# Two graph layers with routed experts on one core: bf16 one-hot rows added before counting, the input normalized on ScalarE, and the first pass reordered

## The chip, the cores and the metric

The kernel runs on one core of a Trainium2 chip. The metric is the device time of one execution in microseconds (us); lower is better. The engines of a core are TensorE (PE; its weight loads are listed as PEld), VectorE (DVE), ScalarE (ACT), GpSimd (POOL) and SyncE (SP). Each works through its own queue in order and waits on semaphores for the others.

## The reference

The input `x` is (128, 64, 256), that is 8192 tokens of 256 numbers in 128 graphs of 64 nodes, with one adjacency matrix a graph. Two layers follow; each normalizes first and adds a residual.

```python
x = x + gnn0(layernorm(x), adj)     # (eps*x + adj@x) @ W1 + b1, rms norm, silu, @ W2 + b2  (256 -> 1024 -> 256)
x = x + ffn0(layernorm(x))          # top 6 of 64 experts, each a 256x256 matrix, softmax weights,
                                    # then a projection, a residual and a layernorm
x = x + gnn1(layernorm(x), adj)     # layernorm, adj@h, two products, relu, residual
x = x + ffn1(layernorm(x))          # top 2 of 8 experts, each 256 -> 512 -> 256 with relu
```

## The kernel before

The kernel makes four passes. The first does `gnn0`, chooses the experts of `ffn0` and writes each token, with its weight and its destination, into rows of a table in DRAM that belong to the chosen expert (until about 700 us). The second fetches pages of 128 rows of one expert each, multiplies them and sends the products back. The third does the rest of `ffn0`, `gnn1` and the routing of `ffn1`; the fourth does the experts of `ffn1`.

The first pass works on 32 blocks of 256 tokens (`T = 2` tiles of 128). `staggered` takes a list of (lag, stage) pairs and in step `s` calls each stage, in the order of the list, for block `s - lag`. So one step holds parts of five blocks: norm and aggregation of block `s+1`, the hidden layer of block `s`, the second product (`project`) of block `s-1`, the residual, second norm, transposes (`turn`) and expert logits (`gate`) of block `s-2`, and the choice and the sending of block `s-3`. PE, DVE and ACT execute in exactly the order in which the stages are written. The framework orders the queues of POOL and SP itself.

The stages that matter here, with the lines of the profile:

- `norm_a`, `norm_s`, `norm_b`: statistics of the input on DVE (L45, L46), reciprocal deviation on ACT (`rstd`, L58, L59), normalized input on DVE (L573). `norm_e` adds the scaled identity to the adjacency tile (L563).
- `hidden(b, j)`, four times: products into one of four PSUM buffers `ph` (L591), then the square of each into `sq` on ACT (L594). `square_sum` adds the eight squares up as a tree on DVE (L601). `rms` sums over partitions on PE (L605), takes the reciprocal root on ACT and loads the table for silu. `scale` multiplies on DVE (L613) and applies silu on ACT (L615).
- `residual_a`, `residual_s`, `residual_b`: residual and statistics on DVE (L630), then six normalized copies of the block, one for each chosen expert, into `xs` (three buffers) on ACT (L643), and two stores.
- `choose`: the eight largest logits and their positions on DVE (L178, L179), then one-hot rows for the six choices (`hot`, 2 x 6 x 64 a partition, L183) by comparing float positions with a table of expert numbers. `weigh` prepares the softmax (L242 on DVE, L243 on ACT) and lets POOL write the destinations (L240).
- `count`: for each of the six choices a product with a strictly upper triangular matrix and one with ones (L191), which count the earlier tokens of each expert.
- `place`: softmax division (`normalize`), bookkeeping, row numbers, 12 sends. The bookkeeping gives experts new chunks of rows once every four blocks: `move_on`, `grow` and `note` run with the blocks whose number is 0, 1 and 2 modulo 4, from block 4 on. Then the counts become places (L267 to L275), the one-hot rows pick each token's row (L277 product, L279 sum, L281 cast) and POOL issues 12 indirect sends (L287).

Three bias rows are split into three bf16 parts each by `row_parts` before the first block (L469 to L476), so that a product with ones can add them. `load_lattice` loads a part of the expert matrices in each of 16 steps.

```python
        staggered(NB, (
            (3, choose), (2, residual_a), ..., (0, lambda b: hidden(b, 0)), (0, lambda b: hidden(b, 1)),
            (2, residual_s), (-1, norm_s), (-1, norm_e), (3, weigh),
            (0, lambda b: hidden(b, 2)), (0, lambda b: hidden(b, 3)), (3, count), (2, residual_b), (-1, norm_b), ...
```

Of the kernel before, what the change touches and what calls it, by code (L numbers as in the profile page):

```python
# [78 lines left out]
class Router:  # L79
# [15 lines left out]
    def __init__(self, tc, pool, small, dram, n, D, E, K, T, pg, S, epoch, name, total=None):  # L95
# [3 lines left out]
        self.epoch, self.EP, self.pitch = epoch, epoch * T * P, S + pg  # L99
# [8 lines left out]
        assert T == 2 and epoch == 4 and n % self.EP == 0 and S % pg == 0 and (5 * T * P <= S or S >= n)  # L108
# [5 lines left out]
        self.expert = self.iota([P, 2 * E], [[1, 2 * E]], 0, "expert")  # L114
        self.page = self.iota([P, 4], [[1, 4]], 4, "page")
# [56 lines left out]
    def choose(self, logits):  # L172

        nc, T, E, K, n = self.nc, self.T, self.E, self.K, self.name
        top = self.small.tile([P, T, 8], F32, name=n + "top")
        idx = self.small.tile([P, T, 8], U32, name=n + "idx")
        for t in range(T):
            nc.vector.max(top[:, t, :], logits[:, t, :])  # L178
            nc.vector.max_index(idx[:, t, :], top[:, t, :], logits[:, t, :])  # L179
        which = self.small.tile([P, T, K], F32, name=n + "which")  # L180
        nc.vector.tensor_copy(which, idx[:, :, :K])
        hot = self.work.tile([P, T, K, E], BF16, name=n + "hot")
        nc.vector.tensor_tensor(hot, self.expert[:, :E].unsqueeze(1).unsqueeze(1).to_broadcast([P, T, K, E]),  # L183
                                which.unsqueeze(3).to_broadcast([P, T, K, E]), op=ALU.is_equal)
        return top, hot

    def count(self, hot):

        for m, lhsT in enumerate((self.tri, self.ones)):
            for k in range(self.K):  # L190
                self.nc.tensor.matmul(self.psum[:, m], lhsT=lhsT, rhs=hot[:, :, k, :],  # L191
                                      start=(k == 0), stop=(k == self.K - 1))
# [15 lines left out]
    def grow(self):  # L208

        v, E = self.nc.vector, self.E  # L210
        t, new, cum = self.t, self.new, self.cum
        v.tensor_sub(t, self.end, self.run[:, 0, :])
        v.scalar_tensor_tensor(new, t, float(self.EP), self.none, op0=ALU.is_lt, op1=ALU.mult)
        v.tensor_tensor_scan(cum, new, self.zero[:, :E], self.used, op0=ALU.add, op1=ALU.add)
        v.tensor_copy(self.used, cum[:, E - 1:E])
        v.tensor_scalar(cum, cum, -1.0, float(self.pitch), op0=ALU.add, op1=ALU.mult)
        v.tensor_sub(t, cum, self.end)
        v.tensor_sub(t, t, self.delta)
        v.tensor_mul(t, t, new)
        v.tensor_add(self.delta, self.delta, t)  # L220
        v.tensor_sub(self.none, self.none, new)
# [37 lines left out]
    def places(self, b, hot):  # L259

        nc, T, E, K, n = self.nc, self.T, self.E, self.K, self.name
        if self.J > 1 and b >= self.epoch and b % self.epoch < 3:
            (self.move_on, self.grow, self.note)[b % self.epoch]()
        pos, cnt = self.psum[:, 0], self.psum[:, 1]
        run = self.run
        self.run = self.counts.tile([P, T, E], F32, name=n + "run")
        nc.vector.tensor_add(run[:, 1, :], run[:, 0, :], cnt[:, 0, :])  # L267
        nc.vector.tensor_add(self.run[:, 0, :], run[:, 1, :], cnt[:, 1, :])
        place = self.work.tile([P, T, E], F32, name=n + "place", bufs=1)
        nc.vector.tensor_add(place, pos, run)  # L270
        if self.J > 1:
            over = self.work.tile([P, T, E], F32, name=n + "over", bufs=1)
            nc.vector.tensor_tensor(over, place, self.end.unsqueeze(1).to_broadcast([P, T, E]), op=ALU.is_ge)
            nc.vector.tensor_mul(over, over, self.delta.unsqueeze(1).to_broadcast([P, T, E]))
            nc.vector.tensor_add(place, place, over)  # L275
        prod = self.work.tile([P, T, K, E], F32, name=n + "prod", bufs=1)
        nc.vector.tensor_mul(prod, hot, place.unsqueeze(2).to_broadcast([P, T, K, E]))  # L277
        row = self.small.tile([P, T, K], F32, name=n + "rowf")
        nc.vector.tensor_reduce(row, prod, op=ALU.add, axis=AX.X)  # L279
        out = self.small.tile([P, T, K], I32, name=n + "row")  # L280
        nc.vector.tensor_copy(out, row)  # L281
        return out
# [129 lines left out]
def two_layer_gnn_moe_kernel(ctx: ExitStack, tc: tile.TileContext, a: dict, out: bass.AP):  # L412
# [49 lines left out]
    def row_parts(pool, name):  # L462

        rest = pool.tile([P, D], F32, name="rest_" + name, bufs=1)
        nc.scalar.dma_start(out=rest, in_=rows_of(a[name]))
        part = small.tile([P, D], BF16, name="part", bufs=1)
        out = const.tile([P, 2, D], BF16, name="p_" + name)
        for i in range(3):
            nc.vector.tensor_copy(part, rest)  # L469
            nc.vector.tensor_sub(rest, rest, part)  # L470
            if i == 0:
                nc.vector.tensor_scalar(out[:, 0, :], part, ident[:, 0:1], None, op0=ALU.mult)
            else:
                nc.vector.scalar_tensor_tensor(out[:, 0, :], part, ident[:, i:i + 1], out[:, 0, :],
                                               op0=ALU.mult, op1=ALU.add)
        nc.vector.tensor_copy(out[:, 1, :], out[:, 0, :])  # L476
        return out
# [20 lines left out]
    r0 = Router(tc, const, small, dram, N, D, E0, K0, T, P, 14 * P, 4, "r0")  # L498
# [22 lines left out]
    with tc.tile_pool(name="c0", bufs=1) as c0, \  # L521
# [27 lines left out]
        rms_w = load_columns(c0, "L0_gnn_rms_weight")  # L549
        w2 = w2_view  # L550
        nc.scalar.dma_start(out=w2, in_=a["L0_gnn_W2"].rearrange("(k p) f -> p k f", p=P))
        gate_wT = load_matrix(c0, "L0_ffn_gate_wT")
        b2 = row_parts(c0, "L0_gnn_b2")
        out_b = row_parts(c0, "L0_ffn_out_b")
        b_rel = row_parts(c0, "L1_gnn_b_rel")

# [10 lines left out]

        def norm_b(b):
            B = blocks[b]
            x, mv, rs = B["x"], B["mv"], B["rs"]  # L570
            B["xn"] = xn = pair[:, b % 2 * T:(b % 2 + 1) * T, :]
            for t in range(T):
                nc.vector.tensor_scalar(xn[:, t, :], x[:, t, :], mv[:, t, 0:1], rs[:, t:t + 1],  # L573
                                        op0=ALU.subtract, op1=ALU.mult)
# [34 lines left out]
        def scale(b):  # L609
            B = blocks[b]  # L610
            B["hT"] = hT = hTs[b % 2]
            for c in range(KH):
                nc.vector.scalar_tensor_tensor(hT[:, c, :], B["ph", c // 2][:, c % 2, :], b1[:, c:c + 1], B["rms"],  # L613
                                               op0=ALU.add, op1=ALU.mult)
                nc.scalar.activation(hT[:, c, :], hT[:, c, :], AF.Silu, scale=rms_w[:, c:c + 1])  # L615
            nc.scalar.preload_act_table_set("natural_log_exp_and_others")

        def project(b, t, lo, hi):
            B = blocks[b]
            if t == 0 and lo == 0:  # L620
                B["po"] = psum.tile([P, T, D], F32, name="ps")
                nc.tensor.matmul(B["po"], lhsT=r0.ones, rhs=b2, start=True, stop=False)
# [12 lines left out]

        def residual_b(b):
            B = blocks[b]
            x1, mv, rs = B["x1"], B["mv1"], B["rs1"]
            nm = small.tile([P, T], F32, name="bn_nm")
            nc.vector.scalar_tensor_tensor(nm, mv[:, :, 0], -1.0, rs, op0=ALU.mult, op1=ALU.mult)  # L640
            B["xs"] = xs = work.tile([P, T, K0, W], F32, name="xs", bufs=3)
            for t in range(T):
                nc.scalar.activation(xs[:, t, :, :D], x1[:, t, :].unsqueeze(1).to_broadcast([P, K0, D]),  # L643
                                     AF.Identity, bias=nm[:, t:t + 1], scale=rs[:, t:t + 1])
            nc.sync.dma_start(out=by_tile(x1_dram[b]), in_=x1)
# [9 lines left out]
        def gate(b):  # L655
            B = blocks[b]
            for t in range(T):
                for k in range(KD):
                    nc.tensor.matmul(pg[:, t, :], lhsT=B["xn1T"][:, k, ts(t, P)], rhs=gate_wT[:, k, :],
                                     start=(k == 0), stop=(k == KD - 1))  # L660

        def choose(b):
            B = blocks[b]
            B["top"], B["hot"] = r0.choose(pg)
# [5 lines left out]
        def count(b):  # L670
            r0.count(blocks[b]["hot"])

        def place(b):
            B = blocks[b]
            r0.normalize(*B["w"], B["xs"])
            r0.send(r0.places(b, B["hot"]), B["xs"])

        def load_lattice(b):
            n = free[0] // 16
            if b < 16:  # L680
                nc.sync.dma_start(out=lat[:, b * n:(b + 1) * n], in_=lat_w[:, b * n:(b + 1) * n])
# [11 lines left out]
            (-1, norm_e),  # L693
            (3, weigh),
            (0, lambda b: hidden(b, 2)),
            (0, lambda b: hidden(b, 3)),
            (3, count),
            (2, residual_b),
            (-1, norm_b),
            (1, lambda b: project(b, 0, 0, 4)),  # L700
            (0, square_sum),
            (-1, aggregate),
            (1, lambda b: project(b, 0, 4, KH)),
            (2, turn),
            (0, rms),
            (3, place),
            (1, lambda b: project(b, 1, 0, KH)),
            (2, gate),
            (0, scale),
            (1, load_lattice),  # L710
# [68 lines left out]
    with tc.tile_pool(name="c3", bufs=1) as c3, \  # L779
# [43 lines left out]
        def out_proj(b):  # L823
            B = blocks[b]
            B["pp"] = pp = po_pool.tile([P, T, D], F32, name="po")
            nc.tensor.matmul(pp, lhsT=r1.ones, rhs=out_b, start=True, stop=False)  # L826
# [68 lines left out]
        def convolve_a(b):  # L895
            B = blocks[b]
            B["pc"] = pc = po_pool.tile([P, T, D], F32, name="pc")
            nc.tensor.matmul(pc, lhsT=r1.ones, rhs=b_rel, start=True, stop=False)  # L898
# [40 lines left out]
        def choose1(b):  # L939
# [3 lines left out]
            top, B["hot"] = r1.choose(logits)  # L943
            r1.compare(b, top, B["xs"])

        def count1(b):
            r1.count(blocks[b]["hot"])
# [5 lines left out]
        def place1(b):  # L953
            B = blocks[b]
            r1.send(r1.places(b, B["hot"]), B["xs"])
# [122 lines left out]
```

## Time and profile before

| | |
|---|---|
| median of 3 runs | 2195.01 us (2194.39 to 2196.17) |
| profiled execution | 2200.25 us, its span 2198.1 us |
| mean granted TensorE clock | 0.962 |
| busy PE / PEld | 88% / 77% of the span |
| busy DVE / ACT / POOL | 54% / 46% / 54% |
| DMA | 398.93 MB, 181 GB/s on average |

The rows of the profile's views give, for a group of instructions, the start, the duration, the engine, the line, the operation and `output<-input` by the tiles' names, with shapes as partitions x elements, and in brackets the idle time before it with what ended that. An `x8` behind a row says that eight like it are merged; the duration is then that of all eight. The view by groups gives a mean in ns. Idle time of an engine that nothing waits for costs nothing. `lat` is a large SBUF tile in which several arrays of the first pass live (`x`, `sq`, `hT`, W1, W2), so many rows name it.

### The profile page before, as it was taken

To read this page: it belongs to the slowest core of one execution; us is meant where nothing else is said; L and a number is where in the kernel's file an instruction comes from. 1 tells how busy PE (TensorE), PEld (TensorE's weight loads), DVE (VectorE), ACT (ScalarE), POOL (GpSimd) and SP (SyncE) were. 2 spreads that over 40 slices of the span, in tenths; PEclk is the share of its full clock that TensorE was granted. 3 is DMA by queue.
4 is the path that set the end of the run, shared out by engine and by line. 5 is a ranking of instruction groups with operands and counts; after the bars stand their busy time and mean duration, and the time that the engine had idled before them with its cause. 6 is when DMAs were issued, how large, how long until landed. Compare 5 with 4: busy or idle time off the path is not lost. (4 is left out here: it accounts for less than half of the span.)

```text
span 2198.1 us, 37431 instructions
## 1 busy us (share of the span) xinstructions
PE 1945.1 (88%) x10563; PEld 1684.8 (77%) x10564; DVE 1186.6 (54%) x3904; ACT 1015.9 (46%) x2037; POOL 1182.8 (54%) x1178
## 2 busy tenths in 40 slices
PE   3999999999961988998898479999996999999997
PEld 2888888888851877887777368888875888888886
DVE  4688888888873333333333248888882222222221
ACT  2887887777750222222222036666662333333332
POOL 1166676666655777777777703333343444434444
PEclk9999999999985999999999789999997999999999
DMA  8143334443364988767675379888835776666665
GB/s 247 56 133 123 129 131 134 133 133 134 127 214 136 282 254 256 210 202 206 206 206 170 92 277 316 265 265 267 262 124 142 179 170 158 162 157 161 162 160 117
DMA packets 283580, 398.93 MB, mean 181 GB/s; under 512 B 56024, under 2 KB 237416, under 8 KB 283376
## 3 DMA queue, kind: packets, MB, share of 16 engines
q1 hardware_dynamic: 200736, 246.15, 38.3%
q0 software_dynamic: 64800, 136.14, 20.8%
q10 hardware_dynamic: 17840, 14.21, 2.0%
q8 instruction: 93, 1.52, 0.3%
q14 instruction: 111, 0.91, 0.2%
HBM read 223.89 MB, written 177.69 MB: 183 GB/s over the span
## 5 line engine op out<-in xcount | busy, mean ns | idle before, releaser
L287 POOL DMA_INDIRECT r0x<-xs,r0row x384 | 397.7, 1036 | 222.2 <-DVE lat L613 100.7
L294 POOL DMA_INDIRECT r0y<-py_s,px x424 | 417.6, 985 | 143.7 <-DMA r0y<-py_s,px 58.2
L758 PE MATMUL py<-lat,pxT 128*128 x1696 | 411.0, 385 | 40.0 <-DVE py_s L763 22.5
L763 DVE TENSOR_SCALAR py_s<-py,px 128x256 f32<-128x256 f32 x424 | 185.6, 479 | 377.4 <-DMA r0y<-py_s,px 158.5
L302 POOL DMA_INDIRECT out_x<-py_s,px x138 | 214.4, 1554 | 312.1 <-DMA out_x<-py_s,px 184.2
L758 PEld LDWEIGHTS py<-lat,pxT 128*128 128x128 f32 x1696 | 307.2, 191 | 91.0 <-issue 31.2
L745 ACT COPY pxT<-pt 128x512 f32<-128x512 f32 x212 | 124.0, 586 | 440.8 <-PE pt L743 309.5
L1017 ACT ACTIVATE phid<-ph,pw 128x256 f32<-128x256 f32 x276 | 131.0, 475 | 325.3 <-issue 178.4
L1015 PE MATMUL ph<-pxT,pw 128*128 128x256 f32 x1104 | 251.4, 381 | 2.1 <-DMA pw<-in_L_ffn_W1b 2.1
L1034 PE MATMUL py<-fw,phid 128*128 x1104 | 249.9, 379 | 0.6 <-ACT phid L1017 0.6
L591 PE MATMUL ph<-lat 128*128 128x256 f32 x1024 | 233.2, 387 | 17.8 <-DVE lat L613 17.1
L624 PE MATMUL ps<-lat 128*128 128x256 f32 x1024 | 237.1, 380 | 0.0
L1015 PEld LDWEIGHTS ph<-pxT,pw 128*128 128x128 f32 x1104 | 211.0, 191 | 31.4 <-issue 2.5
L591 PEld LDWEIGHTS ph<-lat 128*128 128x128 f32 x1024 | 195.2, 193 | 46.9 <-DVE lat L613 17.4
L1034 PEld LDWEIGHTS py<-fw,phid 128*128 128x128 f32 x1104 | 204.4, 190 | 26.0 <-ACT phid L1017 1.0
L624 PEld LDWEIGHTS ps<-lat 128*128 128x128 f32 x1024 | 192.8, 191 | 24.5
L287 POOL DMA_INDIRECT r1x<-xs,r1row x128 | 129.8, 1014 | 115.7 <-ACT xn3T L930 61.9
L743 PE MATMUL pt<-ident,px 128*128 128x128 f32 x848 | 131.8, 277 | 45.0 <-DMA px<-r0x 44.7
L743 PEld LDWEIGHTS pt<-ident,px 128*128 128x128 f32 x848 | 106.8, 143 | 70.9 <-issue 42.9
L1028 DVE TENSOR_SCALAR p<-p 128x2 f32<-128x2 f32 x69 | 12.0, 174 | 240.1 <-ACT p L1027 240.1
L1037 DVE TENSOR_TENSOR py_s<-py,pb 128x512 f32<-128x512 f32 x69 | 47.7, 692 | 157.0 <-PE py L1034 152.0
L615 ACT ACTIVATE lat<-lat,c_L_gnn_rms_weight 128x256 f32<-128x256 f32 x256 | 105.6, 495 | 47.8 <-DVE lat L613 47.7
(264 smaller groups left out, 2866.7 us busy)
## 6 DMA issues: line engine op xcount, KB each, us to landing
px<-r0x SPq DMA_DIRECT2D x424, 129.0 KB
y<-r0y SPq DMA_DIRECT2D x32, 1536.0 KB
pw<-in_L_ffn_W1b SPq DMA_DIRECT2D x69, 514.0 KB
px<-r1x SPq DMA_DIRECT2D x69, 258.0 KB
x<-x SPq DMA_DIRECT2D x64, 256.0 KB
pb<-in_L_ffn_b SPq DMA_DIRECT2D x69, 128.0 KB
r0x<-r0filler ACTq DMA_DIRECT2D x64, 129.0 KB
lat<-in_x SPq DMA_DIRECT2D x32, 256.0 KB
```

The costliest lines, as they stand in the source:

```text
L287: i = self.nc.gpsimd.indirect_dma_start(out=self.table[:, :], out_offset=bass.IndirectOffsetOnAxis(ap=row[:, t, k:k + 1], axis=0), in_=xs[ ...
L294: i = self.nc.gpsimd.indirect_dma_start(out=self.answer[:, :], out_offset=bass.IndirectOffsetOnAxis(ap=x[:, self.D:self.D + 1].bitcast(I32 ...
L302: i, d = f"{self.name}add{i}", self.nc.gpsimd.indirect_dma_start(out=self.total[:, :], out_offset=bass.IndirectOffsetOnAxis(ap=x[:, self.D ...
L591: nc.tensor.matmul(ph[:, c, :], lhsT=w1[:, k, ts(2 * j + c, P)], rhs=B["aggT"][:, k, :], start=(k == 0), stop=(k == KD - 1))
L624: nc.tensor.matmul(B["po"][:, t, :], lhsT=B["hT"][:, c, ts(t, P)], rhs=w2[:, c, :], start=False, stop=(t == T - 1 and c == KH - 1))
L743: nc.tensor.transpose(pt[:, k, ts(q, P)], Q["px", q][:, 0, ts(k, P)], ident)
L745: nc.scalar.copy(xT[:, :, :n * P], pt[:, :, :n * P])
L758: nc.tensor.matmul(py[:, q, :], lhsT=Q["xT"][:, k, ts(q, P)], rhs=lat[:, ds(regs["e"][(2 * j + q) % 4], 1), k, :].rearrange("p o d -> p (o ...
L763: nc.vector.tensor_scalar(y[:, q, :], py[:, q, :], px[:, 0, D + 1:D + 2], None, op0=ALU.mult)
L1015: nc.tensor.matmul(ph, lhsT=w[:, k * F1 + c * P:k * F1 + (c + 1) * P], rhs=Q["xT"][:, k, :], start=(k == 0), stop=(k == KD - 1))
L1017: nc.scalar.activation(hid[:, c, :], ph, AF.Relu, bias=w[:, KD * F1 + c:KD * F1 + c + 1], scale=1.0)
L1034: nc.tensor.matmul(py[:, t, :], lhsT=Q["hid"][:, c, ts(t, P)], rhs=fw2[:, ds(regs["e"][i % 4], 1), c, :].rearrange("p o d -> p (o d)"), st ...
```

## The change

The diff does the following to the shared router and to the first pass.

1. `choose` compares in bf16 with a table `experts` whose last dimension repeats each number three times (`half = K // 2`); the one-hot rows are laid out as 2 x 64 x 3. It then adds the six rows up (`some`, `its`), and `count` makes one product with each matrix instead of six (one instead of two for the second router).
2. The bookkeeping is spread over four blocks: `grow` is cut in two, its second half being `link`, and `note` moves to the blocks that are 3 modulo 4. The room that is kept for an expert grows from four to five blocks, and the chunk of the first router falls from 14 to 13 pages.
3. `place` is cut in two: `spots` (softmax division, bookkeeping, places) stays ahead of the scaling, and `place` (row numbers and sends) goes behind it.
4. The input's normalization moves to ACT, with a small DVE operation for its shift (`norm_n`). The shift of the second norm gets a stage of its own as well (`residual_n`).
5. Of the six copies of a block the first is made in `residual_b`, which now stands between `hidden(b, 2)` and `hidden(b, 3)`; the other five are made by `normalized` behind `norm_b` and behind `aggregate`.
6. `rms` is called ahead of `turn`.
7. The bias rows, W2, the rms weights and the gate weights are loaded after the first `aggregate` (`load_late`), and one row is split in each of the first three steps (`split_late`). `load_lattice` runs eight steps later.

```diff
-        self.epoch, self.EP, self.pitch = epoch, epoch * T * P, S + pg
+        self.epoch, self.EP, self.pitch = epoch, (epoch + 1) * T * P, S + pg
...
+        self.experts = pool.tile([P, E, self.half], BF16, name=name + "experts")
+        nc.vector.tensor_copy(self.experts, self.expert[:, :E].unsqueeze(2).to_broadcast([P, E, self.half]))
...
-        which = self.small.tile([P, T, K], F32, name=n + "which")
-        nc.vector.tensor_copy(which, idx[:, :, :K])
-        hot = self.work.tile([P, T, K, E], BF16, name=n + "hot")
-        nc.vector.tensor_tensor(hot, self.expert[:, :E].unsqueeze(1).unsqueeze(1).to_broadcast([P, T, K, E]),
-                                which.unsqueeze(3).to_broadcast([P, T, K, E]), op=ALU.is_equal)
+        which = self.small.tile([P, T * 2, h], BF16, name=n + "which")
+        nc.vector.tensor_copy(which.rearrange("p (t a) c -> p t (a c)", t=T), idx[:, :, :K])
+        hot = self.work.tile([P, T, 2, E, h], BF16, name=n + "hot")
+        nc.vector.tensor_tensor(hot.rearrange("p t a e c -> p (t a) e c"),
+                                self.experts.unsqueeze(1).to_broadcast([P, T * 2, E, h]),
+                                which.unsqueeze(2).to_broadcast([P, T * 2, E, h]), op=ALU.is_equal)
+        some = self.work.tile([P, T, E, h], BF16, name=n + "some", bufs=1)
+        nc.vector.tensor_add(some..., hot[:, :, 0]..., hot[:, :, 1]...)
+        its = self.work.tile([P, T, E], BF16, name=n + "its")
+        nc.vector.tensor_add(its, some[:, :, :, 0], some[:, :, :, 1])
+        for c in range(2, h):
+            nc.vector.tensor_add(its, its, some[:, :, :, c])
...
         for m, lhsT in enumerate((self.tri, self.ones)):
-            for k in range(self.K):
-                self.nc.tensor.matmul(self.psum[:, m], lhsT=lhsT, rhs=hot[:, :, k, :],
-                                      start=(k == 0), stop=(k == self.K - 1))
+            self.nc.tensor.matmul(self.psum[:, m], lhsT=lhsT, rhs=its, start=True, stop=True)
...
-        if self.J > 1 and b >= self.epoch and b % self.epoch < 3:
-            (self.move_on, self.grow, self.note)[b % self.epoch]()
+        if self.J > 1 and b >= self.epoch:
+            (self.move_on, self.grow, self.link, self.note)[b % self.epoch]()
...
-        nc.vector.tensor_mul(prod, hot, place.unsqueeze(2).to_broadcast([P, T, K, E]))
+        for t in range(T):
+            nc.vector.tensor_mul(prod[:, t], hot[:, t],
+                                 place[:, t, :].unsqueeze(1).unsqueeze(3).to_broadcast([P, 2, E, h]))
...
-    r0 = Router(tc, const, small, dram, N, D, E0, K0, T, P, 14 * P, 4, "r0")
+    r0 = Router(tc, const, small, dram, N, D, E0, K0, T, P, 13 * P, 4, "r0")
...
-                nc.vector.tensor_scalar(xn[:, t, :], x[:, t, :], mv[:, t, 0:1], rs[:, t:t + 1],
-                                        op0=ALU.subtract, op1=ALU.mult)
+                nc.scalar.activation(xn[:, t, :], B["x"][:, t, :], AF.Identity,
+                                     bias=B["nm"][:, t:t + 1], scale=B["rs"][:, t:t + 1])
...
         staggered(NB, (
...
             (-1, norm_e),
+            (2, residual_n),
+            (-1, norm_n),
             (3, weigh),
             (0, lambda b: hidden(b, 2)),
+            (2, residual_b),
             (0, lambda b: hidden(b, 3)),
             (3, count),
-            (2, residual_b),
             (-1, norm_b),
+            (2, lambda b: normalized(b, 0, 1, K0)),
+            (0, split_late),
             (1, lambda b: project(b, 0, 0, 4)),
             (0, square_sum),
             (-1, aggregate),
+            (-1, load_late),
+            (2, lambda b: normalized(b, 1, 1, K0)),
             (1, lambda b: project(b, 0, 4, KH)),
+            (0, rms),
             (2, turn),
-            (0, rms),
-            (3, place),
+            (3, spots),
             (1, lambda b: project(b, 1, 0, KH)),
             (2, gate),
             (0, scale),
+            (3, place),
             (1, load_lattice),
```

## The prediction

> **What bounds the kernel now.** The page first: its slices show the first pass (until about 700 us) with PE and DVE both near nine tenths, so a step has to be walked. The timeline of one engine at a time, over one period of the steady part (from one `choose` to the next, with the `move_on` bookkeeping in it), gives the order. VectorE:
>
> ```profile
> 306.65 0.22 DVE L178 MAX8 r0top<-rms_p 128x8 f32<-128x64 f32 x1
> ...
> 307.97 0.96 DVE L183 TENSOR_TENSOR r0hot<-r0expert,r0which 128x768 bf16<-128x768 f32 x1
> 308.85 0.68 DVE L630 TENSOR_TENSOR x<-ps,lat 128x512 f32<-128x512 f32 x1
> ...
> 312.02 0.16 DVE L242 TENSOR_TENSOR r0w<-r0top 128x12 f32<-128x12 f32 x1
> ...
> 312.40 0.74 DVE L573 TENSOR_SCALAR lat<-lat,bn_mv,rstd 128x256 f32<-128x256 f32 x2
> 313.95 2.49 DVE L601 TENSOR_TENSOR lat<-lat 128x1024 f32<-128x1024 f32 x3 [0.82 <-ACT lat L594]
> ...
> 320.32 0.96 DVE L277 TENSOR_TENSOR r0prod<-r0hot,r0place 128x768 f32<-128x768 bf16 x1
> ...
> 322.38 3.22 DVE L613 SCALAR_TENSOR_TENSOR lat<-ph,c_L_gnn_b,rms 128x256 f32<-128x256 f32 x8
> 325.52 0.22 DVE L178 MAX8 r0top<-rms_p 128x8 f32<-128x64 f32 x1
> ```
>
> The one wait of weight is in front of L601, for ScalarE's squares. ScalarE in the same window:
>
> ```profile
> 312.16 0.20 ACT L59 ACTIVATE rstd<-rstd 128x2 f32<-128x2 f32 x1
> 312.27 0.20 ACT L243 ACTIVATE r0w<-r0w 128x12 f32<-128x12 f32 x1
> 312.37 1.55 ACT L594 ACTIVATE lat<-ph,c_L_gnn_b 128x256 f32<-128x256 f32 x4
> 313.80 3.23 ACT L643 ACTIVATE xs<-x,bn_nm,rstd 128x1536 f32<-128x1536 f32 x2
> ```
>
> The last squares stand behind L243, which waits for L242 on VectorE. So one loop sets the period: VectorE up to L242, ScalarE's exponential and squares, VectorE again. In start-to-start times: choose 2.20, L630 to L563 3.17, L242 to squares 0.35, squares to L601 1.58, L601 tree 2.41, normalize 0.78, move_on 1.50, place rows 1.68, product, sum and cast 2.06, scale 3.14. They add up to 18.87, the whole period. Without bookkeeping that is 17.37; the trace's steps before it starts take 17.35 to 17.37 between first L613s. Bookkeeping adds 1.5, 2.4, 2.05 and 0 over four steps. PE stands still about 1 us a step and is not in the loop.
>
> GpSimd's sends (twelve L287, 1.27 apart, then about 2 us for landing before the next L240) need 17.5 to 18.7 a block (first send to first send, where the rows were ready long before), just under the loop; they end the pass, and PE waits 42 us there. The start, from the timeline of its first 60 us, and the pass end:
>
> ```profile
> 20.12 0.29 DVE L469 CAST part<-rest_L_gnn_b 128x256 bf16<-128x256 f32 x1 [14.02 <-DMA rest_L_gnn_b<-in_L_gnn_b]
> ...
> 35.63 9.95 PE L591 MATMUL ph<-lat 128*128 128x256 f32 x32 [0.68 <-ACT lat L584]
> ...
> 50.72 3.23 DVE L613 SCALAR_TENSOR_TENSOR lat<-ph,c_L_gnn_b,rms 128x256 f32<-128x256 f32 x8 [1.81 <-ACT rms L59]
> ```
> ```profile
> 699.46 0.97 POOL L287 DMA_INDIRECT r0x<-xs,r0row  x1 [0.30 <-issue]
> ...
> 705.01 2.19 PE L743 MATMUL pt<-ident,px 128*128 128x128 f32 x8 [41.92 <-DMA px<-r0x]
> ```
>
> VectorE waits 14 us for a bias row that step 0 does not use.
>
> **The change, part by part.** *Start (late rows).* The first block's adjacency lands at 8.5 by the trace's landing marks, x at 5.3, W1 at 8.1. Without the row splitting the path is 8.5 + L563 0.41 + shift 0.16 + two ScalarE normalizations 1.1 + aggregate 2.07 + copy 0.64, less 0.3 overlap: L591 at about 12.6, 23 earlier. Then `load_late` puts six DMA issues on ScalarE's queue ahead of the squares; the same six take 0.66, 1.89, 0.75, 1.35, 0.71 and 0.36 in the trace, 5.7 together, and each also waits for its semaphore's earlier DMA, behind lattice loads (the built program still issues all 16 of these early on SyncE's queue, so moving `load_lattice` alters little). First squares at 18.3, rstd of block 1 at 20.4, one row split on VectorE (20.12 to 23.47: 3.35), L601 at 24; from L601 to the first L613 4.2 as before (46.50 to 50.72): 28, or 30 with 2 us of semaphore waits. I take −20 (bounds −12, had the issues 8 us of waits, and −23). Steps 1 and 2 each carry another split, with part of it beside the squares, and the first copies: +2.
>
> *One-hot in bf16, rows added.* In the loop: L183's 0.88 slot goes; the compare stays at 0.96 or falls towards bf16 rows (L472, bf16 scalar operation, 0.28 for 256 where f32 L573 has 0.42: 0.53 for 768). It is nearest to L472 in operands: 0.53. First add of 384: 0.34 by that slope, 0.56 by f32 rows. Two adds of 128 with stride: L273's 0.29 each. With 0.03 between dependent ones, choose grows 2.20 → 2.77, +0.57 (bounds +0.3 and +1.2). PE loses ten products of about 0.057, off the loop: 0.
>
> [...]
>
> *ScalarE normalizes the input.* VectorE's 0.74 goes, but it lay inside the wait for the squares: 0. The two ScalarE operations come behind the last squares, off the loop. But `norm_n` now stands before L242 and waits for rstd: it starts where L573 did, 312.40, so L242 moves 312.02 → 312.48, the exponential to 312.67, the squares to 312.77: +0.40.
>
> [...]
>
> *The x1 copies split.* `residual_b` is moved between the squares of hidden 2 and hidden 3. The third pass has its form:
>
> ```profile
> L869 ACT ACTIVATE hn<-x,bn_nm,bn_rs x64: 584/594/604, 1291.3 to 1639.7; 128x256 f32<-128x256 f32 x64
> ```
>
> Two of these with their overlap take 1.0, and L601 waits for the squares behind them: +1.0 (bounds 0.8 and 1.2). Its two stores move ahead of an adjacency load on SyncE that is due a step later: 0. The other five copies follow the squares: ScalarE's own work grows from 15 to 16.5, still under the period.
>
> *Place after scale, bookkeeping in four parts.* VectorE runs in order, so product, sum and cast cost the same after scale; two half products for one, +0.1. Bookkeeping adds 1.5, 1.4, 1.1, 2.05: the same sum. Sends are issued 3.1 later in a step.
>
> *rms ahead of the transposes.* rms was ready at 319.68, scale began at 322.38: 2.7 of cover, gain 0. In the new order rms (behind both copy groups on ScalarE) comes about 14.5 after choose, VectorE at 14.2 plus bookkeeping: +0.35 in steps without it, else 0.
>
> Per step: 0.57 + 0.40 + 1.0 + 0.1 = +2.07, period 19.44 plus bookkeeping. From first L613 of step 3 (100.14) to step 30 (605.14) are 27 steps: +56, and +1 for three without bookkeeping. With a period near 21, GpSimd has 2 us to spare, so the loop, not the sends, carries the growth. The first send of block 27 came 2.5 after that L613; now 3.14 + 2.16 + 0.8 = 6.1: +3.6. From it to the pass end GpSimd's own queue sets 92.8, unchanged.
>
> *Third pass.* PE is full there; two narrow products of about 0.07 fewer in each of 32 steps: −2 (bounds −5 and, if VectorE's extra 0.4 a step took over, +5). Chunk length only alters addresses.
>
> Sum: −20 + 2 + 57 + 3.6 − 2 = +40. The profiled execution is 2200.25 (span 2198.1 and 2.2 around it), giving 2240; it lies 5.2 above the median, so I forecast 2195.0 + 40 = **2235**.
>
> **Rivals.**
> *The copies cost nothing (faster).* ScalarE idles over 3 us a step; if the squares are ready late for another reason, copies and shift fall into that, the loop grows only by 0.6 and −0.7 is won back from VectorE's lighter load. Then the sends at 18.6 a block set the pass: −20 from the start, −3 from 27 steps at 18.6 for 18.7: 2172. It decides below +0.7 a step (20 over 27). For it: ScalarE's 1.92 of waiting before the next step's scaling. Against it: in the built order the copies stand between two pairs of squares that VectorE waits for.
> *The compare stays at 0.96 and the add at 0.56:* +0.65 a step, 18 more: 2253. For it: no two-source bf16 row in the trace.
> *Late loads hold the squares:* start gains 12 instead of 20: 2243.
>
> That a part does not do what it says holds for `load_lattice` alone, and is in the sum.
>
> **How the numbers follow.** Forecast 0.58, slow compare 0.18, late loads 0.13, copies free 0.11. Step bounds of +1.3 to +2.9 give −21 and +22, the start −3 and +8, third pass −3 and +7; together, not all at an end, 2205 to 2264 for the slower cases. The range is 2200 to 2264. About 0.2% (4 us) is what a measurement here can tell from no change. Faster 0.09 is copies-free without its 0.02 near a growth of 0.7; that 0.02 and 0.01 of the others' low tails are same, 0.03; the rest, 0.88, is slower.
>
> **What would show it.** Right: first L613 near 30 us; period 20.5 to 21.5 in bookkeeping steps; wait in front of the tree 2.5 to 3 us; idle GpSimd of 2 us a step; compare near 0.55; third pass a few us shorter. Wrong: a period under 19.4, or sends that run back to back while VectorE waits for their buffers.

## The result, and the profile after

The changed kernel takes 2263.47 us (median of 4, 2260.6 to 2267.8) where the kernel before took 2195.59 (2194.39 to 2197.61): a ratio of 1.031, 95% interval 1.0291 to 1.0328, so 68 us more. The forecast was 2235 with a range of 2200 to 2264: the direction is right, and the time lies at the very edge of the range. The profiled execution spans 2261.6 us for 2198.1. In the runs `warm_steady`, `best` and `start` below, the kernel before, run beside them, itself took 2504.7 us, so their times and steps tell nothing of the sizes in question.

The first scaling (L650) starts at 35.06 us, where it started at 50.72. The first pass ends at 766.96, where it ended at 700.43. Behind that the kernel takes 1494.6 us for 1497.7. So the change is all in the first pass: 15.7 won at the start, and much more lost in the steps.

The timeline of VectorE over one of the new steps answers to the period shown before (start, duration, operation; in brackets the idle time ahead of it and what ended that):

```profile
323.35 3.21 DVE L650 SCALAR_TENSOR_TENSOR lat<-ph,c_L_gnn_b,rms 128x256 f32<-128x256 f32 x8
326.48 1.01 DVE L299 TENSOR_TENSOR r0prod<-r0hot,r0place 128x384 f32<-128x384 bf16 x2
327.52 1.25 DVE L302 TENSOR_REDUCE r0rowf<-r0prod 128x12 f32<-128x768 f32 x1
...
328.90 0.23 DVE L182 MAX8 r0top<-rms_p 128x8 f32<-128x64 f32 x1
...
330.17 0.69 DVE L187 TENSOR_TENSOR r0hot<-r0experts,r0which 128x768 bf16<-128x768 bf16 x1
330.89 0.36 DVE L191 TENSOR_TENSOR r0some<-r0hot 128x384 bf16<-128x384 bf16 x1
...
331.82 0.68 DVE L667 TENSOR_TENSOR x<-ps,lat 128x512 f32<-128x512 f32 x1
...
335.44 0.17 DVE L258 TENSOR_TENSOR r0w<-r0top 128x12 f32<-128x12 f32 x1
338.31 2.41 DVE L638 TENSOR_TENSOR lat<-lat 128x1024 f32<-128x1024 f32 x3 [2.71 <-ACT lat L631]
```

and ScalarE in the same step, with the two copies (L680) between the pairs of squares (L631), as forecast:

```profile
335.64 0.21 ACT L259 ACTIVATE r0w<-r0w 128x12 f32<-128x12 f32 x1 [0.31 <-DVE r0w L258]
335.75 0.82 ACT L631 ACTIVATE lat<-ph,c_L_gnn_b 128x256 f32<-128x256 f32 x2
336.47 1.08 ACT L680 ACTIVATE xs<-x,bn_nm,rstd 128x256 f32<-128x256 f32 x2
337.45 0.83 ACT L631 ACTIVATE lat<-ph,c_L_gnn_b 128x256 f32<-128x256 f32 x2
338.16 1.09 ACT L610 ACTIVATE lat<-lat,bn_nm,rstd 128x256 f32<-128x256 f32 x2
```

This step takes 21.05 us, inside the forecast of 20.5 to 21.5, but the mean of the 27 steps from the first scaling of step 3 to that of step 30 is 21.61. What the step above does not show stands in the waits of VectorE over these 27 steps (us in total, times, longest):

```profile
DVE lat L638 <- ACT lat L631: 73.2, 27, 2.7
DVE lat L650 <- ACT rms L59: 19.1, 18, 2.3
```

The first line is the expected wait for the squares, 27 times 2.7. The second is new: VectorE stands in front of the scaling because rms is late. One of the 18 waits, of 0.6 us, is that of the scaling that opens the first step; the others are in 17 of the 27 steps, 18.5 us together. The windows of two microseconds through such a step, with the busy time of TensorE and its granted clock (the column behind the count), show why:

```profile
356.00:358.00 2.00, 0.15 (x1) 1.00 0.83 304
358.00:360.00 2.00, 0.18 (x1) 0.59 0.45 158
360.00:362.00 2.00, 2.00 (x9) 0.50 0.35 119
362.00:364.00 2.00, 2.00 (x6) 0.50 0.44 134
364.00:366.00 2.00, 2.00 (x10) 0.71 0.41 136
```

TensorE stands still ahead of the aggregation (L618), which waits for the normalized input that ScalarE now makes behind squares and copies; during the pause its clock goes to half, at 358.35, and stays there for 6.83 us. The aggregation and the half of the second product behind it (L661) run in this stretch: 2.14 and 3.59 us, where in the step above, at full clock, they took 1.43 and 1.89. The mean square (L642) behind them starts only at its end, at 365.16. ScalarE in its turn waits 26.2 us for that mean square in the 27 steps, before it can make rms from it. Over the 27 steps of each kernel, in the same columns (length, busy time of TensorE, its weight loads, VectorE, ScalarE and GpSimd, then the clock), of before and of after:

```profile
100.14:605.14 505.00, 477.02 (x2678) 418.54 (x2677) 448.82 (x1355) 405.41 (x784) 345.01 (x350) 1.00 0.39 131
```
```profile
85.72:669.24 583.52, 504.00 (x2412) 434.62 (x2411) 455.65 (x1435) 454.63 (x893) 342.67 (x350) 0.92 0.34 113
```

TensorE has fewer products and is busy 27 us longer. Its waits in these steps have a single line of weight, one pause of 2.7 us or more in each step:

```profile
PE ps L618 <- ACT lat L610: 79.5, 27, 4.2
```

The trace's clock records have no half clock in these steps of before, and in those of after 18 stretches of it, 88.7 us together: ten of 3.41 us and eight of 6.83. The nine steps in which no stretch begins end without a wait for rms, or with at most 0.4 us of one.

The end of the pass is unchanged in kind. GpSimd's last send, and TensorE's wait for the table behind it:

```profile
765.99 0.97 POOL L310 DMA_INDIRECT r0x<-xs,r0row  x1 [0.30 <-issue]
```
```profile
771.61 3.04 PE L797 MATMUL pt<-ident,px 128*128 128x128 f32 x12 [42.01 <-DMA px<-r0x]
```

Means of the 27 steps, in us from one instruction's start on VectorE to the next one's:

| stretch | before | after | difference |
|---|---|---|---|
| scaling | 3.14 | 3.14 | 0 |
| row product, sum, cast | 2.08 | 2.39 | +0.31 |
| choose (largest logits to residual) | 2.19 | 2.92 | +0.73 |
| residual to the adjacency add | 2.86 | 2.86 | 0 |
| adjacency add to the weighing | 0.31 | 0.76 | +0.45 |
| weighing to the tree | 1.97 | 2.87 | +0.90 |
| tree | 2.36 | 2.33 | -0.03 |
| softmax division and bookkeeping | 2.11 | 2.02 | -0.09 |
| place rows, up to the scaling or row product | 1.68 | 2.32 | +0.64 |
| step | 18.70 | 21.61 | +2.91 |

### The profile page after: what moved, and what is told of

It reads as the page before. It is cut to its first block, busy times and chain, and to the rows that moved or that the text cites. A ratio compares the mean times of both kernels' runs of the same rounds, so it can differ in the third digit from the quotient of the medians.

```text
span 2261.6 us, 37011 instructions
## 1 busy us (share of the span) xinstructions
PE 1970.9 (87%) x10180; PEld 1697.8 (75%) x10180; DVE 1200.2 (53%) x4063; ACT 1071.3 (47%) x2165; POOL 1179.7 (52%) x1178
## 4 chain that ended last, share of the span: by engine, by line
PE 41%; DMA 21%; issue 2%; POOL 2%; DVE 1%; ACT 1%; SPq 0%; POOLq 0%; ACTq 0%; DVEq 0%
DMA r0y<-py_s,px 16%; PE ph L1069 10%; PE py L1088 10%; PE py L812 4%; PE ps L872 4%; PE po L883 3%; PE pz L944 3%; PE pc L955 2%; DMA px<-r0x 1%; DMA out_x<-py_s,px 1%; PE pg L990 1%; POOL r0x L310 1%; PE pt L76 1%; PE pc L961 1%; PE ps L76 1%
## 5 line engine op out<-in xcount | busy, mean ns | idle before, releaser
L661 PE MATMUL ps<-lat 128*128 128x256 f32 x1024 | 262.2, 409 | 0.0
L661 PEld LDWEIGHTS ps<-lat 128*128 128x128 f32 x1024 | 208.7, 209 | 29.2
L618 PE MATMUL ps<-at,lat 128*128 128x128 f32 x256 | 58.8, 386 | 97.3 <-ACT lat L610 97.3
L1082 DVE TENSOR_SCALAR p<-p 128x2 f32<-128x2 f32 x69 | 12.6, 183 | 244.0 <-ACT p L1081 244.0
L618 PEld LDWEIGHTS ps<-at,lat 128*128 128x128 f32 x256 | 47.9, 265 | 112.3 <-ACT lat L610 111.9
```

The lines of the kernel that those rows point to most:

```text
L661: nc.tensor.matmul(B["po"][:, t, :], lhsT=B["hT"][:, c, ts(t, P)], rhs=w2[:, c, :], start=False, stop=(t == T - 1 and c == KH - 1))
```

## The experiments

Two theories are set against each other. The loop, as forecast: VectorE and ScalarE in their order make the step, and rms has cover. The clock: TensorE's pause halves its clock, and so rms is late. Where a run's theories differ by less than the later passes differ between executions (1494.6 to 1510.2 us behind the first pass, in the profiled ones of the first eight runs and of after), the mean step decides, not the time. The end of the first pass is given beside it where the time missed its forecast.

**Filling TensorE's pause** (`warm`, the changed kernel with)

```diff
+        def busy(b):
+            for _ in range(16):
+                nc.tensor.matmul(rms_p[:, C + T * E0:], lhsT=mean, rhs=mean, start=True, stop=True)
...
+            (-1, busy),
             (-1, aggregate),
```

> The changed kernel with sixteen 128x128x128 products added per step, ahead of the aggregation on TensorE, into columns of a PSUM bank that nobody reads; they fill the 2.7 us in which TensorE waits for the normalized input and change no other engine's work. Theory (clock): that pause lets the granted clock fall to half for 3.4 or 6.8 us in two steps of three, the aggregation and the half of the second product behind it run at half speed, the mean square behind them comes late and VectorE waits 0.7 us a step for rms. Then the stretches of half clock (99 us of the first pass) go nearly to nothing, VectorE's wait in front of the scaling falls from 19 us to under 4, the step from 21.6 to about 20.9 us, the time to about 2246 (-17). Rival (order): rms is late because it stands behind that half product and the copies at any clock; then the wait stays above 12 us and the time within 5 us of 2263.

Measured: 2261.29 us. In the 27 steps there is no stretch of half clock (the mean granted clock is 1.00), the wait for rms is 5.3 us, 2.7 of it at the scaling that opens the first of them, and the step takes 20.95 us, 0.66 less, as the clock theory said:

```profile
DVE lat L638 <- ACT lat L631: 73.1, 27, 2.7
...
DVE lat L654 <- ACT rms L59: 5.3, 4, 2.7
```

The time missed its forecast of 2246, and the first pass of the profiled execution ends only 9.1 us earlier: from the first scaling to that of step 3 this kernel takes 58.5 us for 50.7, since in the first steps the filling products themselves hold back the aggregation, and VectorE waits 5.6, 4.9 and 2.7 us for rms. The clock's cost in a step is shown; its place in the total is not read from this time.

**rms earlier** (`rms_early`)

```diff
             (-1, load_late),
+            (0, rms),
             (2, lambda b: normalized(b, 1, 1, K0)),
             (1, lambda b: project(b, 0, 4, KH)),
-            (0, rms),
```

> The changed kernel with rms moved directly behind the aggregation, ahead of the second half of the product and of the second group of copies. Theory (clock): the clock still falls as often, but rms now needs only the slow aggregation, is there before VectorE has the places, and the wait of 0.7 us a step goes: 27 steps give -19, about 2244, with the half clock still near 99 us. Rival (the loop alone, as predicted blind): rms had cover and its place is worth nothing; then the time stays within 5 us of 2263.

Measured: 2252.08 us (ratio 1.026, 1.0243 to 1.0277), 11 us less for a forecast of 19; the step takes 20.94, and the first pass ends 20 us earlier (746.91). The half clock is still there, 58.0 us in 14 stretches (88.7 in 18 before this edit), and costs almost nothing, because rms no longer stands behind the product that it slows:

```profile
DVE lat L650 <- ACT rms L59: 0.2, 1, 0.2
```

So the half clock and the place in the queue are both needed for the loss: either one removed takes away the same 0.66.

**The input normalized on VectorE** (`norm_dve`)

```diff
-                nc.scalar.activation(xn[:, t, :], B["x"][:, t, :], AF.Identity,
-                                     bias=B["nm"][:, t:t + 1], scale=B["rs"][:, t:t + 1])
+                nc.vector.tensor_scalar(xn[:, t, :], B["x"][:, t, :], B["mv"][:, t, 0:1], B["rs"][:, t:t + 1],
+                                        op0=ALU.subtract, op1=ALU.mult)
...
-            (-1, norm_n),
```

> The changed kernel with the input normalized by VectorE again, in its old place, and without the shift that stood before the weighing. Blind prediction's terms: the shift's wait goes (0.40 to 0.45 a step), the 0.74 us on VectorE lies in its wait for the squares: -12, about 2251. Theory (clock): the aggregation also no longer waits behind squares and copies on ScalarE, the pause of TensorE falls under 1 us, the clock stays full and the wait for rms goes too: 0.45 + 0.75 = 1.2 us a step, -32, about 2231.

Measured: 2240.21 us (1.0198, 1.0181 to 1.0215), between the two forecasts; the first pass ends 31.3 us earlier (735.62), near the clock theory's 32. The step takes 20.47, 1.14 less: 0.36 in front of the weighing, 0.73 in front of the scaling, where the forecast had 0.40 alone. The half clock falls to 10.2 us in three stretches. The aggregation stands at 35.1 us of TensorE's waits, where it stood at 79.5, and the mean square ahead of rms now waits too:

```profile
PE rms_p L638 <- DVE r0den L271: 40.1, 25, 1.7
PE ps L614 <- issue: 35.1, 24, 1.8
```

So the forecast that the pause falls under 1 us did not come true: TensorE stands still nearly as long in all, but in two pauses of at most 1.8 us a step instead of one of 2.7 or more. The 0.73 us that VectorE does again cost nothing; they lie in its wait for the squares.

**The first copies behind the last squares** (`copies_late`)

```diff
-            (2, residual_b),
             (0, lambda b: hidden(b, 3)),
             (3, count),
+            (2, residual_b),
```

> The changed kernel with the two first copies behind the last squares instead of between them. Blind prediction's term: the squares end 1.0 us earlier in every step, -27, about 2236. Theory (clock): the normalized input still stands behind squares and copies, so TensorE pauses as long, and in the two steps of three with a half clock rms is as late as before and eats the gain; only the third step gains: about -9, 2254, with VectorE's wait for rms grown from 19 to over 30 us.

Measured: 2244.86 us (1.023, 1.0213 to 1.0247); the profiled execution is the slowest of them, with 2267.05, and won 11.2 us in the first pass and lost 14.9 behind it. The time lies between the two forecasts. The step takes 21.20, only 0.41 less, 11 us in 27 steps, which is near the clock theory's 9. Weighing to tree falls by 0.98, as the prediction priced it, and 0.56 of that comes back in front of the scaling:

```profile
DVE lat L638 <- ACT lat L631: 46.8, 27, 1.7
DVE lat L650 <- ACT rms L59: 34.8, 21, 3.3
```

One wait shrinks by 26 us and the other grows by 16. The prediction's price was that of one wait; with the second one behind it, 0.41 us a step is to be had.

**The old one-hot rows in the changed kernel** (`old_onehot`; `choose` and `count` go back likewise)

```diff
-        for t in range(T):
-            nc.vector.tensor_mul(prod[:, t], hot[:, t],
-                                 place[:, t, :].unsqueeze(1).unsqueeze(3).to_broadcast([P, 2, E, h]))
+        nc.vector.tensor_mul(prod, hot, place.unsqueeze(2).to_broadcast([P, T, K, E]))
```

> The changed kernel with the one-hot rows, the counting products and the product and sum of the rows as they were before (compare in f32, twelve counting products, one product of 768). By the measured segments choose falls by 0.73 us and product, sum and cast by 0.31 a step: -28 in 27 steps, +2 in the third pass, about 2237. The ten counting products also shorten TensorE's pause from 2.7 to about 2.1 us; if that is enough to keep the clock, up to 20 us more go, about 2218. Rival (the choice is off the loop): under 10 us of gain.

Measured: 2221.78 us (1.0114, 1.0097 to 1.0131), 42 us less than the changed kernel; the step takes 19.93. Choose falls by 0.77 and the row product by 0.34 a step, and the wait in front of the scaling by 0.58 more, since with the ten counting products back in the pause, now 1.7 us on average (44.9 us in 27 steps), the half clock is down to 20.5 us. Both halves of the expectation came true in the step; the clock is kept for the most part, not wholly.

**Both reversals** (`both`: `norm_dve` and `copies_late`)

> The changed kernel with the input normalized by VectorE and the two first copies behind the last squares. Blind prediction's terms alone: 0.40 + 1.0 a step, -38, about 2225. Theory (clock): with the clock full the wait for rms goes as well, 0.45 + 0.95 + 0.75 = 2.15 a step, -58, about 2205.

Measured: 2213.75 us (1.0077, 1.006 to 1.0094), a step of 19.60, 2.01 less than after; 0.97 in front of the tree, 0.67 in front of the scaling and 0.37 in front of the weighing. The time lies between the two forecasts, the step near that of the clock. With the clock kept, moving the copies is worth 0.87 (20.47 to 19.60), not 0.41.

**The late loads alone** (`late_only`, the kernel before with)

```diff
+        def load_late(b):
+            if b == 0:
+                late["L0_gnn_b2"] = load_rows(c0, "L0_gnn_b2")
...
             (-1, norm_b),
+            (0, split_late),
...
             (-1, aggregate),
+            (-1, load_late),
```

> The kernel before with the late loads and the late, narrower bias rows alone (lattice loads at their old steps). The first scaling was 15.7 us earlier in the changed kernel; if the pass keeps that, 2195.6 - 15 = about 2180. Rival: GpSimd's sends set the pass, and take some of it back, or the splits and the loads in the first steps do: -5 or less.

Measured: 2184.26 us against 2197.4, ratio 0.9935 (0.9918 to 0.9951). The first scaling comes at 35.89, the step is 18.70 as before, and the first pass ends at 686.42, 14.0 us earlier: the pass keeps nearly all of the start. This version beats both kernels.

**The one-hot rows alone** (`onehot_only`, the kernel before with the new `choose`, `count` and row product)

```diff
-            for k in range(self.K):
-                self.nc.tensor.matmul(self.psum[:, m], lhsT=lhsT, rhs=hot[:, :, k, :],
-                                      start=(k == 0), stop=(k == self.K - 1))
+            self.nc.tensor.matmul(self.psum[:, m], lhsT=lhsT, rhs=its, start=True, stop=True)
```

> The kernel before with the bf16 one-hot rows, their adds and the two counting products alone (bias rows kept one row wide to make room). The loop grows by 0.73 for choose and 0.31 for product and sum: +28, less 3 in the third pass, about 2221. Rival: the blind sizes, 0.57 + 0.1 a step, +18 - 3, about 2211. Rival: TensorE loses 0.6 us of work a step, waits longer and loses the clock as well: over 2230.

Measured: 2229.49 us against 2197.4, ratio 1.0141 (1.0125 to 1.0158). The step takes 19.73 for 18.70, so 28 us of the 32 are in the 27 steps; they hold 10.2 us of half clock and no wait of VectorE for rms. The groups in these steps (count, busy time in us, mean ns of one, idle time ahead):

```profile
L293 DVE TENSOR_REDUCE r0rowf<-r0prod 128x12 f32<-128x768 f32 x27 | 31.9, 1181 | 0.9
...
L187 DVE TENSOR_TENSOR r0hot<-r0experts,r0which 128x768 bf16<-128x768 bf16 x27 | 18.7, 692 | 0.9
```

The sum over 768 elements takes 1.18 us where it took 0.95; its shape and types are the same, but its twelve rows now lie interleaved by three; the compare takes 0.69 for 0.96. The third pass took 388.0 us from its first product to its last, 387.9 before and 388.2 in the changed kernel: the 3 us expected there do not exist.

**The filling products from block 4 on** (`warm_steady`, against `warm`)

```diff
-            for _ in range(16):
+            for _ in range(16 if b >= 4 else 0):
```

> The changed kernel with the sixteen filling products only from block 4 on. With them in every step the first three steps grew, since there nothing else holds TensorE back: VectorE waited 5.6, 4.9 and 2.7 us for rms. Theory (clock): without that the steady gain of 0.66 a step stands alone, 27 x 0.66 = 18, about 2245. Rival: the filling products cost elsewhere what the clock brings; then 2255 or more.

Measured: 2612.15 us against 2504.74. The step is 28.86 us and VectorE waits 205.8 us for rms, so the 0.66 in dispute can't be seen. Inconclusive; the first steps did lose most of their extra waits (53.0 us from the first scaling to that of step 3, for 58.5).

**The costly parts taken out together** (`best`, and again as `best_2`; against `both`, with the old functions under names of their own)

```diff
+        if self.half > 1:
+            return self.choose_wide(logits)
...
+        if self.half > 1:
+            return self.places_wide(hot, place)
...
-            r0.count(blocks[b]["its"])
+            r0.count_wide(blocks[b]["hot"])
```

> The changed kernel with the input normalized on VectorE, the first copies behind the last squares, and the first pass's one-hot rows, counting products and row products as before; the second router (two experts a token) keeps the new ones, and the late loads, the four-part bookkeeping and the place behind the scaling stay. By the steps measured one by one: 19.60 - 1.07 = 18.5 us a step, so 27 x 0.2 = 5 below the kernel before, 15 from the start, 3 from the third pass, less 3.9 for the first send and 1 for the first steps: about 2177. Rival: the reverted parts overlap, and the step stays above 18.9: over 2190. Rival: GpSimd's sends hold the step at 18.6 or 18.7: about 2182.

Measured: 2522.32 us against 2504.74; nothing follows. The second time:

> The kernel of the run named best once more, since in that call the kernel before itself took 2504.7 us for 2196. By the steps measured one by one: 19.60 - 1.07 = 18.5 us a step, 27 x 0.2 = 5 below the kernel before, 15 from the start, 3 from the third pass, less 3.9 for the first send and 1 for the first steps: about 2177. Rival: the reverted parts overlap, and the step stays above 18.9: over 2190. Rival: GpSimd's sends hold the step at 18.6 or 18.7: about 2182.

Measured: 2200.51 us against 2199.21, ratio 1.0004 (0.9992 to 1.0015). The sum was wrong. The step is 18.90 for an expected 18.5, and the first pass ends at 699.72. The first rival has the time, but not the cause: against `both`, choose falls by 0.75 and the row product by 0.31 a step, all that was expected of the parts taken out. What the sum lacked stands in front of the scaling, where VectorE waits for rms in 17 of the 27 steps:

```profile
DVE lat L684 <- ACT rms L59: 10.4, 17, 1.8
```

The rival of the sends is right in kind and too small in size: GpSimd's sends start 9 to 10 us behind their rows in the middle of the pass (1 to 5 in `late_only`), one block every 19.4 us on average up to block 27, and ScalarE's copies, which stand ahead of rms, wait for buffers that are still being sent:

```profile
ACT xs L714 <- DMA r0x<-xs,r0row: 22.9, 18, 2.7
```

This wait is not among those of ScalarE in the 27 steps of the changed kernel, whose longer step left GpSimd time: its sends start 0.8 us behind their rows there. That the sends are late because `place` now makes the row numbers behind the scaling is argued, not shown: no run moved it alone.

**The loads behind the squares of block 0** (`start`)

```diff
             (0, lambda b: hidden(b, 3)),
+            (0, load_late),
...
-            (0, split_late),
+            (1, split_late),
```

> The kernel of the run named best with the late loads issued behind the last squares of block 0 instead of ahead of them, and each row split one step later. Theory (ScalarE's queue holds the squares: they were ready at 22 and started at 25.0, behind an issue that stood 6 us): the first scaling comes 4 to 8 us earlier, and the time falls by as much. Rival: the issues then stand ahead of rms on the same queue, and the first scaling stays within 2 us.

Measured: 2521.07 us against 2504.74. The first scaling came at 33.12 for 35.08 in `best` beside it, and the scaling of step 3 at 86.36 for 85.29. That is the rival's side, as far as it can be read.

## Why the prediction was right in direction and short in size

In the two profiled executions the terms compare as follows (us):

| term | forecast | measured | from |
|---|---|---|---|
| start, to the first scaling | -20 | -15.7 | 50.72 and 35.06 |
| steps 0 to 3 | +2 | +1.2 | 49.4 and 50.7 |
| 27 steps | +57 | +78.5 | 505.0 and 583.5 |
| scaling of step 30 to the first send of block 27 | +3.6 | +3.9 | 2.5 and 6.4 |
| that send to the end of the pass | 0 | -1.5 | 92.8 and 91.3 |
| the rest | -2 | -3.1 | 1497.7 and 1494.6 |
| sum | +40 | +63.5 | spans |

**The step that failed is the one for rms ahead of the transposes, "+0.35 in steps without it, else 0" ("it" is the bookkeeping, which 24 of the 27 steps have).** It was worked with a TensorE at full clock and off the loop, since it stood still 1 us a step before. ScalarE's normalization was taken as off the loop as well, with no price for the one who waits for it. In an undisturbed step the arithmetic holds: choose starts at 328.90 and rms ends at 343.37, 14.5 later, as forecast. But the aggregation waits for that normalization behind squares and copies, TensorE pauses 2.7 us or more in every step, the clock halves in two steps of three, and rms, behind the slowed products, comes up to 2.3 us after VectorE. That is 0.64 a step in the segments, 0.66 by `warm` and 0.67 by `rms_early`: 17 to 18 of the 21.5 us that the 27 steps were short. The ten counting products, "off the loop: 0", belong to the same chain: with them back in the pause (`old_onehot`) 0.58 of the wait went. The forecast had named each piece, the moved normalization, the copies and the place of rms, and priced each on its own engine. The price was in the chain across three of them.

**The one-hot terms were mis-sized.** Choose came to +0.73 for +0.57: the compare took 0.69 for the chosen 0.53, inside its bounds of 0.53 and 0.96, and the adds took 0.36, 0.29 and 0.29. Row product, sum and cast came to +0.31 for +0.1: the working counted a second half product and overlooked that the sum's operand had changed its order, over which the sum took 1.22 us for 0.95. Together 0.37 a step, 10 us. The other stretches came out 0.17 a step below their forecast, which takes back some 5 us.

**The range held by luck.** The time is half a microsecond inside its upper end. The step grew by 2.91 for an upper bound of +2.9, but that bound was the sum of a dearer choice (+1.2), dearer copies (+1.2), the shift and the half product; nothing in it stood for a late rms. (The lower bound of +1.3 does not follow from the terms, whose lower ends add up to +1.6.)

**Right:** the squares cut by copies (+0.90 for +1.0; `copies_late` gives 0.98 and `both` 0.97), the shift ahead of the weighing (+0.45 for +0.40), the bookkeeping at the same sum, the late first send, VectorE's normalization as work that had cost nothing. GpSimd did have time to spare in the changed kernel: its sends start 0.8 us behind their rows in all of the 27 steps.

**Start:** -15.7 lies between the forecast and the rival of late loads, which had -12. The first products of the hidden layer start at 12.56, as forecast (12.6), and the late loads then do hold the squares, by 9.0 us for the 5.7 that the prediction had for the six issues. On ScalarE the issues stand from 15.99, there is a hole of 6 us behind the second weight matrix, and the squares of block 0 follow at 25.00, not 18.3:

```profile
16.91 0.59 ACTq L576 DMA_DIRECT2D lat<-in_L_gnn_W  x1
23.43 0.38 ACTq L482 DMA_DIRECT2D m_L_ffn_gate_wT<-in_L_ffn_gate_wT  x1
...
25.00 1.57 ACT L631 ACTIVATE lat<-ph,c_L_gnn_b 128x256 f32<-128x256 f32 x4 [12.49 <-DMA at<-in_adjT]
```

What held the queue in the hole no run shows.

**The rivals:** "the copies cost nothing" fell; the squares behind them cost 26 us in front of the tree (`copies_late`). "The compare stays at 0.96" fell in its cause, and its time of 2253 was nearer than the forecast's 2235 by luck, since other causes made the difference. The third pass gave nothing, for the forecast's -2; the 1.5 and 3 us in the last rows of the table are no larger than the differences between executions of other kernels, and no cause is claimed for them.

Of the parts that a run took by themselves, the late loads alone are worth keeping: -13 us, against +32 for the one-hot rows (28 of them in the 27 steps), +1.1 a step for the normalization on ScalarE and +0.4 to +0.9 a step for the copies between the squares. The bookkeeping in four parts and the place behind the scaling had no run of their own.

## What to carry to other kernels

When work moves to an engine "with time to spare", ask who waits for its result and how long that engine then stands still; here 2.7 us of pause on TensorE were no loss by themselves and cost 0.66 us a step through the clock (`warm`). Price a moved step along the chain that it feeds, with the slower clock as one of the bounds, not engine by engine. And when a change bundles several edits, take them one at a time: one of these gained 13 us, and the sum lost 68.

## What the runs showed that was not expected

- The half clock came behind pauses of TensorE of 1.7 to 4.2 us. In the changed kernel the 18 stretches are in steps with pauses of 2.69 to 4.20 us ahead of the aggregation; the other nine steps, with pauses of 2.69 to 2.79, have none. In `old_onehot` there were six stretches of half clock over 27 steps, behind pauses of 1.7 and 2.1 us; in `norm_dve` three, behind pauses of 1.8; in `onehot_only` three, behind pauses of 1.7; before, with no pause over 1.5, none. Not every such pause does it: `norm_dve` has 49 of up to 1.8 us. What decides between them no run shows.
- The eight stretches of 6.83 us in the changed kernel begin 64.85 us apart, from 163.79 to 617.76, which is three of its mean steps of 21.61. Why they do so no run shows.
- The sum over 768 f32 elements took 0.95 us before, with the summed elements adjacent, and 1.22 in the changed kernel, with a stride of three (means over the 27 steps); in `onehot_only` it took 1.18.
